# Attention scores of one head and key tile as two products of 64 keys instead of one of 128

## The chip, the cores and the metric

The kernel runs on one core of one Trainium2 chip. The metric is the device time in microseconds (us) of one execution on that core, given as the median of several runs. The engines are named as the profile names them: PE is the matrix engine TensorE, PEld its loading of the stationary operand (the profile shows it as an engine of its own), DVE is VectorE, ACT is ScalarE, POOL is GpSimd and SP is SyncE.

## What is computed

Four layers follow one another on an image tensor of 2 images x 128 channels x 64 x 64 pixels (4096 tokens per image), in 32-bit floats. Only layer 0 is touched. Cut to what matters, its reference is:

```python
x_ = biasfree_ln(group_norm(x))
q1, k1, v, q2, k2 = split(depthwise3x3(conv1x1(x_, w_qkv)), 5)   # 4 heads of 32 channels
q1, q2, k1, k2 = (l2norm_tokens(t) for t in (q1, q2, k1, k2))
attn1 = softmax(einsum('bhnc,bhmc->bhnm', q1, k1) * temperature)  # 4096 x 4096 per head
out1 = einsum('bhnm,bhmc->bhnc', attn1, v)
out2 = einsum('bhnc,bhcd->bhnd', v, softmax(channel attention of q2, k2))
x = x + conv1x1(biasfree_ln(conv1x1(out1 + out2, w_po)), w_proj) + b_proj
```

The change is in the product of queries and keys inside attn1.

## The kernel before, in words

The program works on one image after the other in layer 0 (`_layer0`, L1407). For each image it makes the queries, keys and values (`convolutions`, L1627, whose depthwise part at L1546 uses 32x32 pieces of the array), then runs the attention (`attention`, L1750), and folds the output projection of an image into the start of the next image's convolutions (`finish`, L1803). Layers 1 to 3 come after.

The attention keeps four heads side by side: head j lies in the 32 partitions 32j to 32j+31 of `q1` and `k1`. `_attn_four` (L1333) loops over 8 blocks of 512 queries (`qb`) and, inside, over 32 tiles of 128 keys (`kt`). So each image has 256 iterations and the kernel 512. One iteration does this:

- Scores (L1341): two tiles `ps_s` of two PSUM banks each are taken from a pool of three. Four matmuls follow, one for each head, each with 32 rows (the channels of the head) and 128 columns (the keys). Heads 0 and 1 go to the first `ps_s` tile, heads 2 and 3 to the second; below these are called the first and the second half. The four matmuls lie on four different row pieces of the array and run at the same time.
- Exponentials (L1350): ACT takes each `ps_s` tile, 128 x 1024 numbers, into a half of the SBUF tile `weights` (four of these are in use in turn).
- Values (L1757, called from `multiply` at L1774): for the iteration before the present one, four matmuls with 128 rows (the keys) and 32 columns (the channels of a head) add into the accumulator `ps_acc`. They lie on four column pieces and also run at the same time.
- Sums of the exponentials: DVE adds the `weights` tiles of eight iterations together (L1792, seven additions of eight iterations). After that, four matmuls of the same form as the values (`sums`, L1759) add up the partitions, once in eight iterations. At the end of a query block ACT copies two accumulators (L1770 and L1782) and DVE takes a reciprocal (L1771) and multiplies (L1772).

The order on PE is therefore: scores of iteration n, values of n-1, scores of n+1, values of n, and so on. Two waits couple PE and ACT. The values of iteration n need the exponentials of n. The second half of the scores of n+1 goes into the `ps_s` tile that the first half of iteration n had, since three tiles serve two per iteration; so it needs the first exponential of n to have finished. A 32-bit float matmul shows in the trace as two passes, each with a load of the stationary operand (LDWEIGHTS) and a MATMUL record.

The order of instructions on each engine is set by the framework's scheduler here, since the attention isn't in the hand-ordered part (`_in_order`, L1299). Every four iterations one step of side work is mixed in (`_weave`, L115): the small channel attention, the normalization of the next image, and statistics.

Of the kernel before, what the change touches and what calls it, by code (L numbers as in the profile page):

```python
# [18 lines left out]
CH = 512  # L19
# [1313 lines left out]
def _attn_four(nc, p_pool, ps_pool, q, k, multiply):  # L1333

    waiting = []
    for qb in range(NCH):
        for kt in range(NQT):
            ps = [ps_pool.tile([128, 2, CH], F32, tag="sp", name="ps_s") for _ in range(2)]
            for j in range(4):
                rows = slice(32 * j, 32 * j + 32)  # L1340
                nc.tensor.matmul(  # L1341
                    ps[j // 2][:, j % 2, :],
                    k[rows, kt * 128 : (kt + 1) * 128],
                    q[rows, qb * CH : (qb + 1) * CH],
                    start=True,
                    stop=True,
                )
            w = p_pool.tile([128, 4, CH], F32, tag="weights", name="weights")
            for p in range(2):
                nc.scalar.activation(w[:, 2 * p : 2 * p + 2, :], ps[p], AF.Exp)  # L1350
            waiting.append((qb, kt, w))
            if len(waiting) > 1:
                multiply(*waiting.pop(0))
            yield
    for x in waiting:
        multiply(*x)
    yield
# [49 lines left out]
def _layer0(ctx, tc, X, a, cst, worst, there, dram):  # L1407
# [342 lines left out]
    def attention(pool, side):  # L1750
# [23 lines left out]
        def multiply(qb, kt, w):  # L1774
# [22 lines left out]
            if i == SUMMED - 1:  # L1797
                pending.append((qb, kt // SUMMED, parts[0]))

        _weave(_attn_four(nc, pool, spp, q1, k1, multiply), side, 4)  # L1800
        sums()

# [539 lines left out]
```

## Time and profile before

| What | Value |
|---|---|
| median of 3 runs | 4225.66 us (4211.73 to 4226.44) |
| span of the profiled execution | 4221.3 us, mean granted PE clock 0.980 |
| PE busy, whole kernel | 4050.3 us, 96% |
| ACT busy, whole kernel | 3342.7 us, 79% |
| DVE busy, whole kernel | 2186.7 us, 52% |
| layer 0 attention, image 0 | 194.5 to 810.9 us, 256 iterations |
| layer 0 attention, image 1 | 1016.1 to 1605.6 us, 256 iterations |

The profiled execution has no time of its own other than its span; the span lies 4.4 us under the median of the runs and within their spread. A group of the profile gives the line, the engine, the operation, output and input, the piece of the array in rows*columns for PE, and the shape; then count, busy time and the mean of one in ns, and the idle time ahead of it with what ended it. The two attention stretches take 1206 us together, 29% of the span.

### The profile page before, as it was taken

The numbers are of one execution on the slowest core, as the hardware profiler recorded it, in microseconds if no ns is written. First come the engines' busy times: TensorE is split into PE (matmuls) and PEld (weight loads), VectorE is DVE, ScalarE is ACT, GpSimd is POOL, SyncE is SP. The second block draws the span as 40 slices with busy tenths as digits, with TensorE's granted clock in tenths as the row PEclk, the third lists the DMA queues.
The fourth block names the chain that finished last, engine by engine and source line by source line (L and its number), as shares of the span: only waits on it lengthen the run. The fifth ranks groups of instructions, "written<-read, shape, count | busy, mean of one in ns | idle before, by whom it ended". The sixth has DMA issues, their size and how long they took to land. (4 is left out here: it accounts for less than half of the span.)

```text
span 4221.3 us, 82246 instructions
## 1 busy us (share of the span) xinstructions
PE 4050.3 (96%) x35790; PEld 1548.6 (37%) x35790; DVE 2186.7 (52%) x2358; ACT 3342.7 (79%) x4051; POOL 71.6 (2%) x145
## 2 busy tenths in 40 slices
PE   7999999989999998997999999999999999999998
PEld 4523222354222224445664333333333333333332
DVE  4679999757899998986765212221032102211111
ACT  4478888735888883326646999999999999999998
POOL 1001000010000001000000000000000000000000
PEclk9999999999999998998999999999999999999999
DMA  1299950000000000004650000000000000000000
GB/s 48 28 194 191 186 64 1 1 2 2 1 1 1 1 1 12 1 1 170 273 222 4 6 6 4 6 6 6 4 6 6 4 6 6 6 4 6 6 6 5
DMA packets 158822, 158.86 MB, mean 38 GB/s; under 512 B 24809, under 2 KB 148713, under 8 KB 154354
## 3 DMA queue, kind: packets, MB, share of 16 engines
q1 hardware_dynamic: 158450, 153.50, 15.6%
q8 instruction: 282, 4.62, 0.4%
q14 instruction: 90, 0.74, 0.1%
HBM read 145.09 MB, written 73.40 MB: 52 GB/s over the span
## 5 line engine op out<-in xcount | busy, mean ns | idle before, releaser
L2104 ACT ACTIVATE weights<-ps_s 128x1024 f32<-128x1024 f32 x2048 | 1885.2, 1104 | 65.9 <-PE ps_s L2094 65.4
L1350 ACT ACTIVATE weights<-ps_s 128x1024 f32<-128x1024 f32 x1024 | 992.8, 1022 | 178.6 <-PE ps_s L1341 154.0
L2113 PE MATMUL ps_acc<-weights,vt 128*32 128x512 f32 x8192 | 1095.5, 607 | 0.0
L2094 PE MATMUL ps_s<-q,k 32*128 32x512 f32 x8192 | 925.8, 445 | 5.2 <-ACT weights L2104 5.2
L1792 DVE TENSOR_TENSOR sums<-sums,weights 128x2048 f32<-128x2048 f32 x384 | 879.2, 2289 | 43.1 <-ACT weights L1350 8.2
L2094 PEld LDWEIGHTS ps_s<-q,k 32*128 32x128 f32 x8192 | 472.7, 183 | 842.0 <-ACT weights L2104 775.2
L1341 PE MATMUL ps_s<-q,k 32*128 32x512 f32 x4096 | 649.3, 643 | 3.7 <-ACT weights L1350 1.3
L2135 DVE COPY u<-ps_acc 128x512 f32<-128x512 f32 x32 | 22.1, 692 | 1041.3 <-PE ps_acc L2113 1041.3
L1757 PE MATMUL ps_acc<-weights,vt 128*32 128x512 f32 x4096 | 550.4, 607 | 3.4 <-ACT used L1782 3.2
L1341 PEld LDWEIGHTS ps_s<-q,k 32*128 32x128 f32 x4096 | 210.5, 184 | 431.4 <-issue 212.9
L2113 PEld LDWEIGHTS ps_acc<-weights,vt 128*32 128x32 f32 x8192 | 163.1, 108 | 378.4 <-issue 366.5
L1757 PEld LDWEIGHTS ps_acc<-weights,vt 128*32 128x32 f32 x4096 | 81.1, 108 | 396.6 <-issue 378.4
L662 DVE SCALAR_TENSOR_TENSOR X<-g,w,X 128x2048 f32<-128x2048 f32 x84 | 197.4, 2351 | 2.6
L1792 DVE TENSOR_TENSOR sums<-weights 128x2048 f32<-128x2048 f32 x64 | 146.5, 2290 | 65.2 <-ACT weights L1350 65.2
L1546 PE MATMUL ps_sp<-pad,diag 32*32 32x512 f32 x4608 | 159.7, 599 | 2.3 <-ACT q L1566 1.3
L1008 PE MATMUL ps_z<-w_ri,e 128*32 128x128 f32 x2048 | 137.4, 409 | 14.6 <-DVE e L950 12.2
L2055 DVE TENSOR_TENSOR vt<-ps_acc,bv 128x384 f32<-128x384 f32 x32 | 17.8, 557 | 247.0 <-PE ps_acc L2048 247.0
L2025 DVE LOAD_MASK_SELECT qq<-ps_acc x32 | 0.4, 14 | 222.5 <-PE ps_acc L2022 222.5
L1546 PEld LDWEIGHTS ps_sp<-pad,diag 32*32 32x32 f32 x4608 | 95.0, 103 | 55.6 <-issue 17.7
L2138 DVE RECIPROCAL r<-r 128x512 f32<-128x512 f32 x32 | 107.3, 3354 | 1.1
L950 DVE TENSOR_SCALAR e<-ps_pe 32x136 f32<-32x136 f32 (+1 forms) x352 | 104.4, 297 | 4.9
L948 ACT ACTIVATE e<-ps_pe 32x136 f32<-32x136 f32 (+1 forms) x352 | 99.4, 282 | 4.1
(288 smaller groups left out, 2586.4 us busy)
## 6 DMA issues: line engine op xcount, KB each, us to landing
w_ri<-w_r SPq DMA_DIRECT2D x16, 2112.0 KB, 8.1
w_ri<-w_i SPq DMA_DIRECT2D x16, 2112.0 KB, 13.7
w_r<-in_L_conv_kr_w SPq DMA_DIRECT2D x15, 528.0 KB, 12.7
w_r<-in_L_conv_kr_x SPq DMA_DIRECT2D x15, 528.0 KB, 12.5
w_r<-in_L_conv_kr_y SPq DMA_DIRECT2D x15, 528.0 KB, 12.3
w_r<-in_L_conv_kr_z SPq DMA_DIRECT2D x15, 528.0 KB, 12.6
w_i<-in_L_conv_ki_w SPq DMA_DIRECT2D x15, 528.0 KB, 12.6
w_i<-in_L_conv_ki_x SPq DMA_DIRECT2D x15, 528.0 KB, 12.5
```

Source lines behind the costliest of these rows:

```text
L662: nc.vector.scalar_tensor_tensor(xi, g[:, i : i + H // 2, j : j + W], w8[:, s : s + 1], xi, ALU.mult, ALU.add)
L950: nc.vector.tensor_scalar_mul(out, got[of, :, s], sign)
L1008: nc.tensor.matmul(out.rearrange("p (n f o) -> p n f o", n=2, f=2), e[:, s, 2 * j : 2 * j + 2, :].rearrange("p f x -> p (f x)"), w.rearran ...
L1341: nc.tensor.matmul(ps[j // 2][:, j % 2, :], k[rows, kt * 128 : (kt + 1) * 128], q[rows, qb * CH : (qb + 1) * CH], start=True, stop=True,)
L1350: nc.scalar.activation(w[:, 2 * p : 2 * p + 2, :], ps[p], AF.Exp)
L1546: nc.tensor.matmul(ps[r // 2][to, r % 2, :].rearrange("p (h w) -> p h w", w=W), diag[rows, grp, t, :], pad[rows, y0 : y0 + ROWS, t % 3 : t ...
L1757: nc.tensor.matmul(ac[n][rows, :], lhs(rows), w[:, j, :], start=first, stop=last)
L1792: nc.vector.tensor_add(parts[0].rearrange("p j c -> p (j c)"), t.rearrange("p j c -> p (j c)"), w.rearrange("p j c -> p (j c)"),)
L2094: nc.tensor.matmul(ps[j // 2][:, j % 2, :], k[rows, kt * 128 : (kt + 1) * 128], q[n][rows, qb * CH : (qb + 1) * CH], start=(n == 0), stop= ...
L2104: nc.scalar.activation(w[p], ps[p], AF.Exp)
L2113: nc.tensor.matmul(ac[0][32 * j : 32 * j + 32, :], vt[:, kt, j // 2, i : i + 2, :].rearrange("p a d -> p (a d)"), w[j // 2][:, i, :], star ...
L2138: nc.vector.reciprocal(r, r)
```

## The change

Each scores matmul is split into two: the first makes the scores of keys 0 to 63 of the tile and writes PSUM partitions 0 to 63, the second those of keys 64 to 127 and partitions 64 to 127. Both stream the same 512 queries. There are eight matmuls on 32x64 pieces of the array in place of four on 32x128. Everything else is as it was; the lines after the change move down by two, and the scores are at L1343.

```diff
             for j in range(4):
                 rows = slice(32 * j, 32 * j + 32)
-                nc.tensor.matmul(
-                    ps[j // 2][:, j % 2, :],
-                    k[rows, kt * 128 : (kt + 1) * 128],
-                    q[rows, qb * CH : (qb + 1) * CH],
-                    start=True,
-                    stop=True,
-                )
+                for half in range(2):
+                    to = slice(64 * half, 64 * half + 64)
+                    nc.tensor.matmul(
+                        ps[j // 2][to, j % 2, :],
+                        k[rows, kt * 128 + 64 * half : kt * 128 + 64 * half + 64],
+                        q[rows, qb * CH : (qb + 1) * CH],
+                        start=True,
+                        stop=True,
+                    )
             w = p_pool.tile([128, 4, CH], F32, tag="weights", name="weights")
```

## The prediction

> **What bounds the kernel now.** I read the page first, then the stretches by windows, then the waits and the order of time inside one stretch. The page's groups of the layer 0 attention:
>
> ```profile
> L1350 ACT ACTIVATE weights<-ps_s 128x1024 f32<-128x1024 f32 x1024 | 992.8, 1022 | 178.6 <-PE ps_s L1341 154.0
> L1341 PE MATMUL ps_s<-q,k 32*128 32x512 f32 x4096 | 649.3, 643 | 3.7 <-ACT weights L1350 1.3
> L1757 PE MATMUL ps_acc<-weights,vt 128*32 128x512 f32 x4096 | 550.4, 607 | 3.4 <-ACT used L1782 3.2
> L1341 PEld LDWEIGHTS ps_s<-q,k 32*128 32x128 f32 x4096 | 210.5, 184 | 431.4 <-issue 212.9
> ```
>
> ACT stood idle 154.0 us of this stage for the scores, so it is not the bound; PE is hardly ever idle in the trace. The windows give a quiet query block (no side work) and the waits view 447 to 593 us of it:
>
> ```profile
> 447.40:520.10 72.70, 72.44 (x546) 18.88 (x544) 67.61 (x31) 62.97 (x66) 0.00 (x0) 1.00 1.04 188
> ```
>
> ```profile
> ACT weights L1350 <- PE ps_s L1341: 16.1, 32, 1.2
> ```
>
> The columns of the first are length, then PE, PEld, DVE, ACT and POOL busy. 72.70 us for 32 iterations are 2.272 us each. ACT waits for scores 32 times in 64 iterations: every second one. Why every second is seen in order of time:
>
> ```profile
> 407.89 0.31 PEld L1341 LDWEIGHTS ps_s<-q,k 32*128 32x128 f32 x8 [0.84 <-issue]
> 407.89 1.14 PE L1341 MATMUL ps_s<-q,k 32*128 32x512 f32 x8
> 408.96 0.16 PEld L1757 LDWEIGHTS ps_acc<-weights,vt 128*32 128x32 f32 x8 [0.76 <-issue]
> ...
> 409.06 4.01 ACT L1350 ACTIVATE weights<-ps_s 128x1024 f32<-128x1024 f32 x4 [0.36 <-PE ps_s L1341]
> ...
> 409.95 0.48 PEld L1341 LDWEIGHTS ps_s<-q,k 32*128 32x128 f32 x8 [0.84 <-PE ps_s L1341]
> 409.96 1.31 PE L1341 MATMUL ps_s<-q,k 32*128 32x512 f32 x8
> ...
> 411.20 0.16 PEld L1757 LDWEIGHTS ps_acc<-weights,vt 128*32 128x32 f32 x8 [0.76 <-issue]
> ...
> 412.19 0.31 PEld L1341 LDWEIGHTS ps_s<-q,k 32*128 32x128 f32 x8 [0.84 <-issue]
> ```
>
> Scores start at 407.89, values at 408.96, scores at 409.95. These second scores last 0.17 us longer (1.31 against 1.14; loads 0.48 against 0.31): their second half waits for the exponential that began at 409.06. So a ring sets the pace, over two iterations. Exponential of the first half begins (409.06); 1.07 us later it has freed its tile and the second half of the next scores starts; 1.06 us later the values start (411.20); 0.99 us later the next scores (412.19); 1.18 us later the next such exponential begins (413.37 in the same view). Sum 4.30 us. Eight iterations are four times 4.30 plus 0.96 us for the extra sum matmuls: 18.17 us, or 2.27 per iteration, which is the 72.70 above.
>
> **What the Trainium skill says.** "TensorE: Matmul & The Clock Gate", section "LDWEIGHTS (loading the stationary operand)": the load takes columns divided by 1.2 ns, whatever the rows. The trace agrees: loads of 128 columns last 181 ns at least, of 32 columns 106, so 75 ns for 96 columns, 0.8 ns each. In its Part 3 (packing), tiles start some 4 ns apart; here it is 7: four scores matmuls of 0.692 us each end 0.71 us after the first began. The same part says that a load overlaps running matmuls only when the row group differs. The values differ from that: four matmuls that all use 128 rows start 7 ns apart (0.64 us for four of 0.617). "TensorEngine Tiling (Array Packing)", section "Key Properties": a change of tiling mode drains the array. The trace shows some 0.52 us from the last second pass's start to the next group's first load, alike behind scores and values. The kernel changes mode twice per iteration before and after, so this stays.
>
> **The change part by part.** The order of instructions on every engine is the same in the built kernel after, but for each scores matmul standing twice; no DMA is added, and the waits stay on the first matmul of each half, so no wait is added or moved.
>
> *Shorter load.* The first load of a group is bare, since the array has just been drained: the second pass of the scores begins 0.53 us after the first (408.42 after 407.89 in a narrower window of the same view), that of the values 0.45 us after it (409.41 after 408.96). The difference of 78 ns is that of 128 and 32 columns. With 64 columns the start is 64 x 0.8 = 51 ns shorter. The second pass's load lies beside the first pass and is free.
>
> *More starts.* 2048 more matmuls, each of two passes. A half has four starts instead of two, so its last start comes 3 x 7 = 21 ns after its first instead of 7: 14 ns more. That eight or more pieces can stream at once at full rate is seen in the depthwise convolution, 16 pieces of 32x32:
>
> ```profile
> 922.69 0.72 PE L1546 MATMUL ps_sp<-pad,diag 32*32 32x512 f32 x16 [0.32 <-ACT q L1566]
> ```
>
> Sixteen first passes of 0.61 us end within 0.72 us, so again 7 ns apart, and the second passes begin at 923.15, 0.455 us after those of the same piece: no slower than the values. Queueing the extra instructions is hidden behind the 0.99 us of the values, which are already in the array; if that cover fails, see the second case.
>
> *Sum.* The ring has two legs with a bare load: second half to values (1.06) and scores to exponential (1.18). Each loses 51 - 14 = 37 ns, so two iterations lose 74 and one loses 37. The PE path without the wait is 1.07 + 0.99 = 2.06 us and goes down by 51 - 4 x 7 = 23 ns, to 2.04; twice this is 4.08, under the ring's 4.23. ACT needs four exponentials per two iterations, 4.01 us by the view (3.94 us at 404.76, since the records overlap), so ACT stays under 4.23 as well. 512 x 0.037 = 18.9 us.
>
> *What does not come through.* Five of the 16 query blocks carry side work and take longer: by windows 84 us for the first, 94 and 75 for the next two, and 78 and 75 in image 1, in place of 72.7. There DVE, POOL and side matmuls hold the iteration in part; I credit half of 160 x 0.037 = 5.9, so 3.0 us are lost (bounds 0 and 5.9). DVE is next in line: it is busy 67.6 of 72.7 us, and after a reciprocal (3.35 us) it runs late. In the trace the closest it comes is 0.33 us ahead of the exponential that needs the `weights` tile back, some nine iterations after the reciprocal; 9 x 0.037 = 0.33 uses this up, so I take 0.03 to 0.1 us per block, about 1 us. Total: 18.9 - 3.0 - 1.0 = 15 us off. The span of 4221.3 would be 4206; against the median, 4225.7 - 15 = 4210.7. Bounds of this case: no loss and starts without the 14 ns give 512 x 0.051 = 26 us off (4200); all losses and 10 ns per start, 7 us off (4219).
>
> **The rivals.**
> 1. *The starts are dearer.* Inside a depthwise run of 288 records a tap takes 9.75 us less 0.6, over nine: 1.02, where two passes are 0.86. The 0.16 over 16 matmuls are 10 ns on top of each 7. At 17 ns the last start of a half is at 51 instead of 7: a leg loses 51 - 44 = 7, 3.6 us in all: 4222. For it: instructions arrive at that pace when none are queued. Against: at the head of a group, as here, 7 ns are seen.
> 2. *Two loads in one row group go one after the other* (slower). The skill's sentence would allow it, and the order in the loop puts both halves of a head next to each other, on the same rows. Then starts lie at 0, 51, 58, 109 ns in the first half and up to 225 in the second. A leg gains 102 - 51 = 51 ns; PE's own path grows by 225 - 21 - 51 = 153 to 2.21 us, 4.43 for two, which now passes the ring's 4.40. That is 0.13 over 4.30, so 0.065 per iteration, and 33 us: 4259. It turns slower once the last start of a half is more than 58 ns behind its first. Against it: the values' loads share all rows and start 7 ns apart. For it: no 64-column piece is in the trace, and the depthwise loop takes another row at each step, so this order is not shown there.
> 3. *The bare load is no time on the ring, or DVE takes all of it*: 4226. Against it speaks the 0.53 against 0.45 us, and DVE's 5 us of slack per block.
>
> **How the numbers follow.** Forecast 0.57, rival 1 0.17, rival 2 0.21, rival 3 0.05. About 0.5% (21 us) is what a measurement of this kernel can tell from no change. The forecast's own range 4200 to 4219 lies about that line: 0.21 of its 0.57 I give to more than 21 us off, since runs of one kernel here differ by 15 us, and 0.36 to within. With rivals 1 and 3, within is 0.58; rival 2 is slower, 0.21. The range reaches from the forecast's lower bound to a little past rival 2: 4198 to 4263.
>
> **What would show it.** Right: second pass 0.48 us after the first in the scores; loads of some 130 ns; quiet blocks at about 71.5 us; eight starts within 0.05 us. Rival 1: eight starts over 0.12 us, blocks at 72.5. Rival 2: starts in steps of 51 ns, blocks at 74.8, and the wait of ACT for scores grown. Wrong in general: if 32x64 pieces stream at a slower rate than both kinds of pieces seen here, the second pass begins later than 0.53 us and all of this fails.

## The result, and the profile after

| | before | after |
|---|---|---|
| median | 4219.62 us (20 runs, 4207.87 to 4229.67) | 4209.94 us (20 runs, 4197.9 to 4214.29) |
| span of the first profile | 4221.3 us | 4206.8 us |
| quiet query block (32 iterations) | 72.71 us | 71.80 us |
| attention, image 0 and 1, first profile | 616.3 and 589.5 us | 609.0 and 582.7 us |

The ratio is 0.9975, with a 95% interval of 0.9968 to 0.9981: 10.5 us off, 8 to 13.5. A repeat with 21 runs (e7 below) gave 0.9976. The kernel is faster by less than 0.5%; 15 us off and 4210.7 us had been forecast.

The page's groups of the attention, after. The last column is the idle time ahead of the group and what ended it:

```profile
L1352 ACT ACTIVATE weights<-ps_s 128x1024 f32<-128x1024 f32 x1024 | 992.9, 1022 | 163.9 <-PE ps_s L1343 144.4
L1343 PE MATMUL ps_s<-q,k 32*64 32x512 f32 x8192 | 633.4, 616 | 4.8 <-ACT weights L1352 1.5
L1759 PE MATMUL ps_acc<-weights,vt 128*32 128x512 f32 x4096 | 549.9, 606 | 3.9 <-ACT used L1784 3.7
L1343 PEld LDWEIGHTS ps_s<-q,k 32*64 32x64 f32 x8192 | 162.2, 130 | 437.0 <-PE ps_s L1343 337.9
```

There are twice as many matmuls and loads, yet the scores' busy time went from 649.3 to 633.4 us: the pieces stream together. A load takes 130 ns in place of 184. ACT's wait for scores fell from 154.0 to 144.4 us only, and the scores still end it.

A quiet block by windows (length, then PE, PEld, DVE, ACT and POOL busy; third from the end the granted clock of PE), and the order of time in one:

```profile
515.76:587.56 71.80, 71.49 (x804) 16.04 (x800) 67.63 (x31) 62.96 (x67) 0.00 (x0) 1.00 0.96 136
```

```profile
530.67 0.23 PEld L1343 LDWEIGHTS ps_s<-q,k 32*64 32x64 f32 x16 [0.84 <-PE ps_s L1343]
530.68 1.11 PE L1343 MATMUL ps_s<-q,k 32*64 32x512 f32 x16
531.72 0.16 PEld L1759 LDWEIGHTS ps_acc<-weights,vt 128*32 128x32 f32 x8 [0.81 <-issue]
...
531.83 3.98 ACT L1352 ACTIVATE weights<-ps_s 128x1024 f32<-128x1024 f32 x4 [0.33 <-PE ps_s L1343]
532.71 0.40 PEld L1343 LDWEIGHTS ps_s<-q,k 32*64 32x64 f32 x16 [0.84 <-PE ps_s L1343]
532.72 1.28 PE L1343 MATMUL ps_s<-q,k 32*64 32x512 f32 x16
...
533.92 0.16 PEld L1759 LDWEIGHTS ps_acc<-weights,vt 128*32 128x32 f32 x8 [0.81 <-issue]
...
534.92 0.23 PEld L1343 LDWEIGHTS ps_s<-q,k 32*64 32x64 f32 x16 [0.84 <-PE ps_s L1343]
...
536.07 1.94 ACT L1352 ACTIVATE weights<-ps_s 128x1024 f32<-128x1024 f32 x2 [0.27 <-PE ps_s L1343]
```

The pattern is that of before. Every second group of scores still waits in its middle (loads 0.40 instead of 0.23 us, scores 1.28 instead of 1.11). From exponential to exponential over two iterations it is 536.07 - 531.83 = 4.24 us, where it was 4.30. From single records, the four legs of that ring are, as medians over some 60 rounds:

| leg | before | after |
|---|---|---|
| first-half exponential to second half of the next scores | 1.075 us | 1.075 us |
| second half to values | 1.057 | 1.018 |
| values to next scores | 0.996 | 0.996 |
| scores to first-half exponential | 1.176 | 1.156 |

So 0.059 us went from two iterations. It came from the two legs that the prediction named, but not in equal parts: 0.039 and 0.020.

### The profile page after: what moved, and what is told of

Same layout as the page of the kernel before. It is cut to its first block, busy times and chain, and to the rows that moved or that the text cites. A ratio compares the mean times of both kernels' runs of the same rounds, so it can differ in the third digit from the quotient of the medians.

```text
span 4206.8 us, 90438 instructions
## 1 busy us (share of the span) xinstructions
PE 4031.8 (96%) x39886; PEld 1502.7 (36%) x39886; DVE 2187.1 (52%) x2358; ACT 3342.6 (79%) x4051; POOL 71.6 (2%) x145
## 5 line engine op out<-in xcount | busy, mean ns | idle before, releaser
L1352 ACT ACTIVATE weights<-ps_s 128x1024 f32<-128x1024 f32 x1024 | 992.9, 1022 | 163.9 <-PE ps_s L1343 144.4
L2096 PE MATMUL ps_s<-q,k 32*128 32x512 f32 x8192 | 926.1, 445 | 5.3 <-ACT weights L2106 5.3
L2096 PEld LDWEIGHTS ps_s<-q,k 32*128 32x128 f32 x8192 | 472.8, 183 | 841.8 <-ACT weights L2106 775.2
L1343 PE MATMUL ps_s<-q,k 32*64 32x512 f32 x8192 | 633.4, 616 | 4.8 <-ACT weights L1352 1.5
L1343 PEld LDWEIGHTS ps_s<-q,k 32*64 32x64 f32 x8192 | 162.2, 130 | 437.0 <-PE ps_s L1343 337.9
L1548 PEld LDWEIGHTS ps_sp<-pad,diag 32*32 32x32 f32 x4608 | 96.2, 103 | 54.6 <-issue 17.1
```

Of the source, the lines that this page charges most:

```text
L1343: nc.tensor.matmul(ps[j // 2][to, j % 2, :], k[rows, kt * 128 + 64 * half : kt * 128 + 64 * half + 64], q[rows, qb * CH : (qb + 1) * CH], ...
L1548: nc.tensor.matmul(ps[r // 2][to, r % 2, :].rearrange("p (h w) -> p h w", w=W), diag[rows, grp, t, :], pad[rows, y0 : y0 + ROWS, t % 3 : t ...
L2096: nc.tensor.matmul(ps[j // 2][:, j % 2, :], k[rows, kt * 128 : (kt + 1) * 128], q[n][rows, qb * CH : (qb + 1) * CH], start=(n == 0), stop= ...
```

## The experiments

Two theories stood against each other for where the gain arises. **The ring**: the pace is set by the chain of the table above, and only what lies on it counts. **The sum of work**: PE is always busy, and each shorter scores group gives the same. A third question was what the added matmuls cost.

### Splitting one kind of iteration only (e1, e2)

In the quiet blocks the scores that wait are nearly always those of the even key tiles (154 of 165 in the first profile after). The edit, for even tiles (for odd ones, `kt % 2 == 1`), from the kernel before:

```diff
-                nc.tensor.matmul(
-                    ps[j // 2][:, j % 2, :],
-                    k[rows, kt * 128 : (kt + 1) * 128],
...
+                n = 2 if kt % 2 == 0 else 1
+                for half in range(n):
+                    m = 128 // n
+                    to = slice(m * half, m * half + m)
+                    nc.tensor.matmul(
+                        ps[j // 2][to, j % 2, :],
+                        k[rows, kt * 128 + m * half : kt * 128 + m * half + m],
...
```

> Only key tiles of even number are split into 64 keys; odd ones stay one product of 128. Ring theory (pace set by: first-half exponential, second half of the next scores, values, next scores, first-half exponential): the scores that wait are those of even tiles, so only the leg from second half to values is shortened, by 0.040 us per two iterations. Quiet query block of 32 iterations: 72.71 - 16 x 0.040 = 72.07 us; whole kernel 512/2 x 0.040 = 10 us off, ratio 0.9976. Rival (PE's own sum of work sets the pace, every split scores group gives the same): half of the change's whole effect, block 72.25 us, the same for even and odd.

> Only key tiles of odd number are split. Ring theory: these scores don't wait, they are on the ring only by the leg from their start to the first-half exponential, which the change shortened by 0.020 us (1.176 to 1.156). Quiet block 72.71 - 16 x 0.020 = 72.39 us, 5 us off, ratio 0.9988. Rival (PE's sum of work): block 72.25 us, as with even tiles.

A quiet block of the kernel with even tiles split:

```profile
517.37:589.49 72.12, 71.85 (x676) 17.29 (x672) 67.62 (x31) 62.96 (x66) 0.00 (x0) 1.00 0.82 112
```

The same with odd tiles split:

```profile
517.56:589.96 72.40, 72.11 (x674) 17.70 (x672) 67.62 (x31) 62.99 (x67) 0.00 (x0) 1.00 0.79 104
```

72.12 and 72.40 us, against 72.07 and 72.39 by the ring and 72.25 twice by the sum of work. The same number of matmuls was split, and one place gave 0.59 us, the other 0.31. The ring holds, and the sum of work, which asks for two equal parts, does not; together they make 0.90 of the change's 0.91. In the first, the leg to the values is 1.018 us and the leg from unsplit scores to the exponential 1.176; in the second, 1.057 and 1.156. Each leg changed just where the edit touched it. The two attentions together tell the same: 1197.1 us in e1 and 1200.4 in e2, which is 8.7 and 5.4 less than the 1205.8 of the first profile before (all three had equally long stretches of lowered clock there, 17.1 us); the sum is the 14.1 of the change. The time of the whole kernel tells less: ratios 0.9989 (0.9982 to 0.9996) and 0.9995 (0.9987 to 1.0003), where 0.9976 and 0.9988 had been expected. The order is right, but the first misses its number, and the second can't be told from no change; what lies between is taken up below.

### Smaller pieces still (e3)

The edit is that of e1 with `n = 4` always: sixteen matmuls on 32x32 pieces.

> Scores as four products of 32 keys on 32x32 pieces, sixteen matmuls per iteration. Theory that the bare load gives and the starts take: load 26 ns shorter again; a half has eight starts, its last 27 ns later; leg from second half to values about 1.02 us (unchanged from the change); leg from start to exponential 1.156 - 0.026 + 0.027 + about 0.04 of longer completion (10 ns for each matmul more in the half, from 1.156 against the 1.136 that load and starts alone give) = 1.20 us. Quiet block 72.71 - 16 x 0.02 = 72.4 us, worse than the change's 71.80, ratio 0.9988. Rival (only the load counts): 26 ns off each leg, block 71.0 us, ratio 0.9955. Rival (starts are dearer when there are many, 17 ns each): block above 73.5 us, slower than before.

A quiet block, and a group of scores in it in order of time:

```profile
517.09:589.64 72.55, 72.25 (x1320) 15.75 (x1312) 67.62 (x31) 63.02 (x66) 0.00 (x0) 1.00 0.86 137
```

```profile
532.14 0.25 PEld L1345 LDWEIGHTS ps_s<-q,k 32*32 32x32 f32 x32 [0.84 <-PE ps_s L1345]
532.14 1.16 PE L1345 MATMUL ps_s<-q,k 32*32 32x512 f32 x32
533.23 0.16 PEld L1761 LDWEIGHTS ps_acc<-weights,vt 128*32 128x32 f32 x8 [0.84 <-issue]
533.23 1.06 PE L1761 MATMUL ps_acc<-weights,vt 128*32 128x512 f32 x8
533.34 1.94 ACT L1354 ACTIVATE weights<-ps_s 128x1024 f32<-128x1024 f32 x2 [0.33 <-PE ps_s L1345]
```

72.55 us: nearly all is lost again, though the loads are shortest (103 ns mean in the groups). The ratio is 0.9999 (0.9991 to 1.0008). Both gains are smaller than expected (72.4 us and 0.9988), though the legs came out as forecast: from scores to exponential it is now 533.34 - 532.14 = 1.20 us (median 1.196, expected 1.20); from second half to values 1.022 (1.02). What the block loses beside them stays open. The two rival numbers, 71.0 and above 73.5, are both out.

The price of one more matmul can be read here. In the trace the last second pass of the first half starts 0.541, 0.502 and 0.502 us after the scores began, for 2, 4 and 8 matmuls in the half. From there to the exponential it takes 0.635, 0.654 and 0.694 us: a straight line, 10 ns for each matmul in the half. The records of the semaphore (the signal that ACT waits for) show that this time passes on PE's side: the signal comes 0.612, 0.632 and 0.672 us after that start, and ACT begins 0.02 us after the signal in all three. So a matmul costs 7 ns at its start on both legs, and 10 ns more at its end on the leg where ACT waits for the half to be complete.

### Heads in turn (e4)

```diff
-            for j in range(4):
-                rows = slice(32 * j, 32 * j + 32)
-                for half in range(2):
-                    to = slice(64 * half, 64 * half + 64)
+            for p in range(2):
+                for half in range(2):
+                    to = slice(64 * half, 64 * half + 64)
+                    for j in (2 * p, 2 * p + 1):
+                        rows = slice(32 * j, 32 * j + 32)
...
```

> As the change, but in each half the two heads take turns, so that neighbouring matmuls lie on different rows of the array. If loads in one row group stood in each other's way, this order would gain over the change, the 0.020 us of longer completion at least: block 71.5 us. If they don't, nothing moves: block 71.80 us, ratio 0.9975.

```profile
513.49:585.28 71.79, 71.49 (x804) 16.04 (x800) 67.62 (x31) 62.94 (x66) 0.00 (x0) 1.00 0.97 136
```

A quiet block took 71.79 us and the legs are the change's to the ns (1.018 and 1.156). Nothing moves: two neighbouring loads on the same rows of the array don't stand in each other's way. The ratio was 0.9986 (0.9979 to 0.9992), less gain than expected of the same attention (0.9975); this too is taken up below.

### Split in one half only (e6)

The edit is that of e1 with `n = 2 if j >= 2 else 1`: heads 0 and 1 stay on 32x128 pieces, heads 2 and 3 go to 32x64.

> Only heads 2 and 3 (the second half) are split into 64 keys, heads 0 and 1 stay on 32x128 pieces. If a change between 32x128 and 32x64 pieces drains the array like that between scores and values, the second half starts some 0.5 us late: scores take 1.07 + 0.5 us or more, an iteration 2.27 + 0.4 or more, 512 x 0.4 = 200 us slower, ratio 1.05. If it doesn't, the leg from second half to values is 0.040 us shorter and the leg to the exponential as before: block 72.07 us, ratio 0.9976.

```profile
614.20:715.90 101.70, 101.70 (x676) 22.24 (x680) 67.80 (x31) 66.51 (x67) 0.00 (x0) 1.00 0.00 1
```

```profile
529.75 1.02 ACT L1354 ACTIVATE weights<-ps_s 128x1024 f32<-128x1024 f32 x1
...
530.60 0.30 PEld L1345 LDWEIGHTS ps_s<-q,k 32*128 32x128 f32 x4 [0.84 <-PE ps_s L1345]
530.61 2.15 PE L1345 MATMUL ps_s<-q,k 32*128 32x512 f32 x12
...
531.66 0.21 PEld L1345 LDWEIGHTS ps_s<-q,k 32*64 32x64 f32 x8 [0.76 <-issue]
531.78 2.06 ACT L1354 ACTIVATE weights<-ps_s 128x1024 f32<-128x1024 f32 x2 [1.01 <-PE ps_s L1345]
...
532.68 0.16 PEld L1761 LDWEIGHTS ps_acc<-weights,vt 128*32 128x32 f32 x8 [0.81 <-issue]
```

In order of time, the second half's first load comes 1.06 us after the first half's (531.66 after 530.60), as late as values come after scores. It did not wait for its tile: the exponentials before it had ended by 530.77 (529.75 + 1.02). The halves no longer run together: scores take 2.08 us, a quiet block 101.70 us, the kernel 1.1046 (1.1029 to 1.1063) of the time before. Here only the column width changes, from 128 to 64, and the two halves lie on different rows, yet the second half comes as late as after a change of tiling. The Trainium skill, "TensorEngine Tiling (Array Packing)", section "Key Properties", says that any change of tiling mode drains the array; this trace agrees. The expectation had a floor of 0.4 us per iteration; it is (101.70 - 72.71) / 32 = 0.91.

This run also tells what the end of a half depends on. Each half is alone in the array here, and still it is 1.177 us from the start of two wide matmuls to their exponential and 1.157 us from the start of four narrow ones to theirs (medians over 402 iterations), as with the other half running beside them (1.176 and 1.156). So the matmuls of the half count, not all that run.

### Where 4 of 14 us went (e5, e7 to e12)

The attention of the first pair of profiles is 14.2 us shorter, the medians differ by 9.7. So both kernels were run again, unedited.

> The kernel before, unchanged, to have a second profile of it. The first profile was 14.5 us longer than that of the change, the medians differ by 9.7 us. If the attention stretches take 616.3 and 589.5 us again, the gain there is 14 us in every run and the rest of a median's difference arises elsewhere; if they are shorter here by some 4 us, the first profile overstated the gain. Ratio 1.000.

> The changed kernel, unedited, together with the kernel before on one chip. By the attention stretches of the profiles it should be 14 us (0.34%) faster, ratio 0.9966; the first comparison gave 0.9975 and the same attention stretches with heads in turn gave 0.9986. If the ring is all, the ratio is 0.9966 and the earlier ones are scatter of the chips; if something outside the attention gives back a part, the ratio stays near 0.998 and the stages outside the attention are longer in this profile than in that of the kernel before.

> The kernel before once more, on the chip and in the rounds of the run above, for a third profile of it. Ratio 1.000; attention blocks of 72.71 us; the parts outside the attention differ from those of the other two profiles of it (3015 us each) by no more than some 5 us.

> The kernel before, for the length of its stages only. Question: the attention stretches of the change are 14 us shorter, the medians only 10 us. If a stage outside the attention gives 4 us back, it is longer in every profile of the change than in every one of the kernel before; the stretch between the two attentions is the candidate (202.9 to 205.3 us so far in the kernel before). If it is scatter, the stages outside overlap.

> The change, for the length of its stages only: the stretch between the two attentions was 205.5 and 205.6 us so far. Giving back: again above those of the kernel before, and the parts outside together some 4 us longer. Scatter: overlapping.

> The kernel before, one more look at the length of its stages. Giving back: the stretch between the two attentions below 205.5 us once more. Scatter: anywhere from 202 to 206 us.

> The change, one more look at the length of its stages. Giving back: the stretch between the two attentions at 205.5 us or more once more. Scatter: anywhere from 202 to 206 us.

Ratios: e5 1.0003 (0.9994 to 1.0013), e8 1.0007 (0.9997 to 1.0017), e7 0.9976 (0.9968 to 0.9983). e7 thus gave the smaller gain again and not the 0.9966 of the attention alone. The last four runs are single executions. The quiet blocks are 72.71 in each of five profiles before, and 71.79 or 71.80 us in each of four after. By stages:

| us | before, five profiles | after, four profiles | difference of the means |
|---|---|---|---|
| both attentions | 1203.6 to 1205.8, mean 1204.35 | 1189.5 to 1191.7, mean 1190.6 | -13.75 |
| between them | 201.3 to 205.3, mean 203.1 | 205.4 to 205.6, mean 205.5 | +2.5 |
| after them | 2610.6 to 2617.7, mean 2614.4 | 2615.6 to 2620.0, mean 2617.7 | +3.3, overlapping |

The stretch between the attentions (the end of image 0's layer and the convolutions of image 1) runs the same instructions in both. By windows, the kernel before in its second profile:

```profile
809.30:1012.10 202.80, 174.27 (x2765) 107.41 (x2764) 111.48 (x172) 75.91 (x130) 13.48 (x40) 0.97 0.01 2
```

The change in its second profile:

```profile
801.70:1007.30 205.60, 178.19 (x2775) 109.24 (x2776) 111.74 (x172) 75.90 (x131) 13.45 (x40) 0.95 0.01 2
```

DVE, ACT and POOL are busy equally long; PE is busy 3.9 us longer, and the granted clock (third from the end) is 0.95 in place of 0.97. The clock records say how: PE ran at half clock for 20.5 us in each of the four profiles of the change, and for 10.2, 13.7, 13.7, 13.7 and 20.5 us in those of the kernel before, always in pieces of 3.4 or 6.8 us. No kernel here edits this stretch, and its length follows this time in all of them: 201.3 and 201.4 us where 10.2 us ran at half clock (one profile before, and e3), 202.8 to 203.8 at 13.7 us (three profiles before, e1, e6), 205.3 to 205.7 at 20.5 us (one profile before, the four of the change, e2, e4). So 2.5 us of the gain are given back here by the clock. Why the clock falls so is argued only: in the first profiles of both kernels and in e5 the pieces start on a grid of 3.413 us, which fits the window of 3413 ns in the Trainium skill, "TensorE: Matmul & The Clock Gate", Part 1, and an attention that ends at another phase of it would meet the grid otherwise. The first profile before, at 20.5 us, shows that it isn't bound to the kernel. e12, at 205.4 us, fell just short of the 205.5 that had been asked of it. With the stretch, 13.75 - 2.5 = 11.3 us remain, within the measured 8 to 13.5.

Half clock falls into image 0's attention too, for 10.2 to 17.1 us. Profiles with the same time of it give 1205.8 against 1191.6 and 1191.7 us (at 17.1), and 1203.6 against 1189.5 and 1189.6 (at 10.2): 14.1 us both times, which is the gain of the attention at an equal clock. In the stages after the attentions the lengths overlap, but there too the shortest, 2610.6 and 2610.9, had 108 us of half clock and the longest, 2620.0, had 136.5. On average it is 119.2 us before and 126.5 after, so a part of the 3.3 us may be the clock's; whether the edit brings it about stays open.

The granted clock of the single runs points the same way. Its mean is 0.9821, 0.9816 and 0.9813 over the comparison runs of the kernel before (55, 19 and 34 runs, on three chips), 0.9803 and 0.9804 for the change (20 and 21 runs) and 0.9799 with heads in turn. Among the runs of one kernel on the chip of e1 to e4, a clock lower by 0.001 goes with a time longer by 2.4 us. An estimate at equal clock, from straight lines through the runs of each chip, is 12.6 us off for the change (e7) and for heads in turn, 8.2 for e1, 2.4 for e2 and 0.9 for e3. By this estimate most of what e1 lacked, and all of what heads in turn lacked, goes with the lower clock; why the edited kernels are granted less is not shown.

## Why the prediction was right, by its steps

- **The ring sets the pace**: held. e1 and e2 give unequal parts, as the ring says and the sum of work does not.
- **The bare load is 51 ns shorter**: held. The shortest loads are 127 ns against 181, and the second pass starts 0.480 us after the first (521.269 to 521.749), as forecast.
- **Starts 7 ns apart, no row-group trouble, no slower streaming**: held for the starts, and eight of them lie within 0.05 us; the second pass at 0.480 us speaks against slower streaming, though the ends cost more, as the next point says. The second rival (4259 us) fell with e4 and with the first records of the change.
- **Each of two legs loses 37 ns**: here the size was off. The leg to the values lost 39. The leg to the exponential lost 20, since the term "4 matmuls in a half instead of 2" had been priced at starts only, 14 ns; it measured 14 at the starts and 20 at the ends. That 7 and 10 make the first rival's 17 ns per matmul is chance: it had put the 10 at the starts, on both legs, and left 7 ns of gain to each. Two iterations gained 59 ns instead of 74, and 512 iterations would gain 15.1 us instead of 18.9.
- **What does not come through, 4 us**: the losses named were too large. DVE took nothing: after the reciprocal it still ends 0.09 us ahead of the exponential that needs its tile (0.33 before), so it is nearly the next in line, but no wait arose. The blocks with side work gained 0.5 to 1.0 us each where they repeat (83.6 to 83.1, 75.68 to 74.72, 77.75 to 77.13, 75.58 to 74.87), where half of a quiet block's gain would be 0.46.
- **The sum, 15 us**: 13.75 in the attention, 14.1 at an equal clock. Too large a gain and too large a loss cancelled in part, which is luck. What the clock takes back, 2.5 us between the attentions at least, was not thought of; the kernel gained 10.5 us and not 15, and 15 lies beyond the measured 8 to 13.5. That the forecast time of 4210.7 us still met the measured 4209.94 within 1 us is luck as well: its base, a median of 3 runs (4225.66), lay 6 us above that of the 20 runs (4219.62).

## What to carry to other kernels

Where a group of matmuls follows a change of the array's tiling, its first weight load is bare and worth shortening; split the columns only as far as the added matmuls cost less than the load saves, which here was at two pieces and no longer at four. Look for the chain that closes on itself over two iterations before pricing a stage: the same edit was worth twice as much in the waiting iteration as in the other. And keep one tiling for all matmuls that are to run together.

## What was not expected of the hardware

The end of a group of matmuls costs more the more of them there are: 10 ns for each, with one signal for the whole half. The Trainium skill, "TensorE: Matmul & The Clock Gate", section "The cost: per-tile semaphore tail", has a term of 4.7 ns for each tile; here it is twice that for a matmul, but a matmul is two records in the trace, and for each of these it is 5 ns. The runs don't tell whether it goes by matmuls or by records. And a stage that no edit touches was 2.5 us longer on average, as PE was granted half clock for 6.1 us more (20.5 us against a mean of 14.3).
